# Sparse graph attention on one core: order of the setup, of the first softmax and of the last group's stores, and one lag for the V products

## The chip, the core and the metric

The kernel runs on one core of a Trainium2 chip. A core has five engines that run side by side, each with its own queue of instructions, taken in order: TensorE (PE, with its weight loads as PEld), VectorE (DVE), ScalarE (ACT), GpSimd (POOL) and SyncE (SP). SyncE, ScalarE and GpSimd can issue DMAs. The metric is the device time of one execution in microseconds; the time of a kernel is the median of several executions.

## What is computed

A graph of 3327 nodes with 256 features each goes through four layers. `adj` has about 0.5% ones, some 16 neighbours a row. Layer 0 is a graph attention whose score depends on the row alone; layers 1 to 3 are transformer layers with 8 heads of 32, in which node n attends to its neighbours only.

```
# layer 0
h = x @ Wt.T + bt
s = leaky_relu(h @ Wa.T + ba)                      # one number a row
w = softmax(where(adj > 0, s, -9e15), axis=1)
x = layernorm(x + (w @ h) @ Wp.T + bp)
# layers 1, 2, 3
q, k, v = split(layer_norm(x) @ w_qkv)
scores  = where(adj != 0, q @ k.T / sqrt(32), -inf)   # for each head
x = x + (softmax(scores) @ v) @ w_proj + b_proj
x = x + gelu(layer_norm(x) @ w1 + b1) @ w2 + b2
```

## The kernel before

The rows are 26 blocks of 128, in 7 groups of four blocks (the last group has two). All instructions are in an order written out by hand: what stands first in the program on an engine is issued first there, and waits for its inputs with everything behind it waiting too. The kernel has two stages.

**Setup and adjacency (first 470 us).** For each block i of `adj`: `load` brings its 128 rows in (SyncE), `sign` turns them into bf16 0/1 on ScalarE (L722; three buffers), `turn` transposes them with 26 matmuls on TensorE and four copies on ScalarE (L731, L732), `candidates` and `list` find the neighbours' numbers on VectorE (L743, L747; L753 to L760). `sums(i)` multiplies the turned pair of blocks with h, split in bf16 parts, on TensorE (L869, L871).

Before the loop, x itself has to be turned and multiplied into h: for each group `x_turn(g)` (L803, copies L805) and one step later `h_of(g - 1)` (matmuls L813, an add on VectorE L819). Between these steps stand `pieces`: the candidates and lists of blocks 2, 3 and 4, cut into five pieces each, for VectorE. `turn(3)` stands after group 2's step, `sign` of block 4 in group 4's. Then come `sum_h` (L840), `split_h` (L828 to L834), `sums(1)`, `turn(4)`, `sums(3)`, the copy of group 0's sums, `turn(5)`, `back` of group 0 and `sums(5)`.

In the loop, i goes from 4 to 25; each i has a first half (load and sign of block i + 2, then the steps of `plan[2 * i]`, candidates of block i) and a second (turn of block i + 2, sums after every second one, the steps of `plan[2 * i + 1]`, list of block i). The plan spreads what each group needs after its sums: copy and back (ScalarE and TensorE), `soft` (small VectorE operations L903 to L932 and two exps on ScalarE, L933 and L934), `mix` (VectorE, L952 to L964, needs the exps), `place`, `project` (TensorE s_ptn and s_pp, ScalarE s_nT), `add` (VectorE, L985, needs s_pp), norms, `turn1` and the products for Q, K and V of layer 1 (`qkv`, L1023), and `store`. Group 0 has all its steps one half later than the other groups.

After the loop the last two groups are finished. `store` and `qkv` put K and V rows into the table kv[1] (L1029) and the rows of x, Q and neighbour lists into the table t1 (L1035, L1036); ScalarE issues these DMAs. Block ranks by degree give the permutation `perm` (L1199 to L1207); `wide` carries the ranks into kv[1] (L1171, ScalarE).

**Layers 1 to 3.** GpSimd gathers rows of kv by neighbour number, four neighbours of 128 nodes at a time: a tile `kv` of a ring of 10 buffers (L1325, four gathers a tile; in layer 1 also 26 gathers of t1's rows, L1285). For each tile, `scores` multiplies with Q and reduces on VectorE (L1347, L1348). After a block's last tile `softmax` finds the maximum on VectorE (L1359) and takes the exp on ScalarE (L1362), followed there by `take_q` of the next block (L1333). Later `weights` (L1368 to L1375) and, for each tile, `values` multiply V with the weights on VectorE (L1388) and add up on TensorE (L1394) into po; that frees the tile and lets GpSimd gather the next one (`issue`). `block` then projects (L1418) and adds (L1422); every few blocks a `chunk` runs the norm, the feed-forward part (L1462, L1468, L1485, L1499, L1503) and the next layer's Q, K, V (L1515, L1521 to L1523) in steps that `some` hands out after each tile. After all blocks the next layer's gathers start, since they read rows that this layer wrote.

When the V products of a block may start is set in `run`: at least one tile of the next block must have been scored in the last layer and for block 0, at least two elsewhere. One V product is done for each scored tile, two when more than five tiles wait for theirs.

Of the kernel before, what the change touches and what calls it, by code (L numbers as in the profile page):

```python
# [8 lines left out]
FP = mybir.dt.float32  # L9
BF = mybir.dt.bfloat16  # L10
I32 = mybir.dt.int32
# [6 lines left out]
P = 128  # L18
N = 3327
D = 256  # L20
HEADS = 8
HD = D // HEADS
# [26 lines left out]
LMAX = CAPS[0]  # L49
# [474 lines left out]
def sparse_path(ctx, tc, ins, out, dram, flag):  # L524
    nc = tc.nc
# [15 lines left out]
    t1 = dram.tile([PADDED, T1W], FP, name="t1")  # L541
    kv = {1: dram.tile([PADDED + 1, KVW[1]], FP, name="kv1"),
          2: dram.tile([PADDED, KVW[2]], FP, name="kv2"),
          3: dram.tile([PADDED, KVW[3]], FP, name="kv3")}
# [21 lines left out]
    class Norm:  # L566
# [18 lines left out]
        def turn(self, j, v, work, pb):  # L585

            xn = work.tile([P, D], FP, tag="xn", name=f"xn_{self.name}_{j}")
            nc.scalar.activation(xn, v, AF.Identity, bias=self.nm[:, j:j + 1],  # L588
                                 scale=self.rs[:, j:j + 1])
            for c in range(2):  # L590
                nc.tensor.transpose(pb[c][:, j * P:(j + 1) * P], xn[:, c * P:(c + 1) * P], ident)  # L591
# [31 lines left out]
    with tc.tile_pool(name="a", bufs=1) as a, tc.tile_pool(name="aw", bufs=2) as aw, \  # L623
# [4 lines left out]
        def bank(name):  # L628
            return a_ps.tile([P, 512], FP, tag="bank", name=name)
# [25 lines left out]
        x_sb = a.tile([P, NB, D], FP, name="s_x")  # L655
# [27 lines left out]
        lists = a.tile([P, NB, LMAX], FP, name="lists")  # L683
# [124 lines left out]
        def h_of(g):  # L808
            blocks, xT = GROUPS[g], turned.pop(g)
            ph = bank(f"s_ph_{g}").rearrange("p (b h) -> p b h", h=H0)  # L810
            for j, i in enumerate(blocks):
                for c in range(2):
                    nc.tensor.matmul(ph[:, j, :], xT[:, c, j * P:(j + 1) * P],  # L813
                                     S.wtT[:, c, :], start=(c == 0), stop=(c == 1))
            full = [j for j, i in enumerate(blocks) if ROWS[i] == P]
            for j0, j1, r in ((0, len(full), P), (len(full), len(blocks), ROWS[-1])):
                if j1 > j0:
                    i0 = blocks[j0]
                    nc.vector.tensor_add(  # L819
                        S.h[:r, i0:i0 + j1 - j0, :], ph[:r, j0:j1, :],  # L820
                        S.bt_b[:r, None, :].to_broadcast([r, j1 - j0, H0]))
# [14 lines left out]
        def sum_h():  # L836
            ph = bank("s_phsum")
            for i in range(NB):
                r = ROWS[i]
                nc.tensor.matmul(ph[:, :H0], ones[:r, :], S.h[:r, i, :],  # L840
                                 start=(i == 0), stop=(i == NB - 1))
            S.hsum = a.tile([P, H0], FP, name="s_hsum")
            nc.scalar.copy(S.hsum, ph[:, :H0])
# [11 lines left out]
        class Group:  # L855
# [150 lines left out]
            def turn1(self):  # L1006
# [4 lines left out]
                    self.n1.turn(j, x_sb[:, i, :], aw, pb)  # L1011
                self.n1.out(self.hT, pb, S.w1["g1"], S.w1["be1"])

            def qkv(self, j0):

                if j0 == 0:
                    self.ql = aw.tile([P, 4, D + LMAX], FP, tag="ql", name=f"ql_{self.g}")
                for j in range(j0, min(j0 + 2, self.n)):
                    i = self.blocks[j]
                    pk, pq = bank(f"s_pk_{i}"), bank(f"s_pq_{i}")  # L1020
                    for ps, c0, c1 in ((pk, D, 3 * D), (pq, 0, D)):
                        for c in range(2):
                            nc.tensor.matmul(ps[:, :c1 - c0], self.hT[:, c, j * P:(j + 1) * P],  # L1023
                                             S.w1["w_qkv"][:, c, c0:c1],
                                             start=(c == 0), stop=(c == 1))
                    kvr = aw.tile([P, 2 * D], FP, tag="kvr", name=f"s_kvr_{i}")
                    nc.scalar.copy(kvr, pk)
                    nc.scalar.mul(self.ql[:, j, :D], pq[:, :D], -HD ** -0.5)
                    nc.scalar.dma_start(kv[1][1 + i * P:1 + (i + 1) * P, :2 * D], kvr)  # L1029
# [11 lines left out]
        groups = [Group(g) for g in range(len(GROUPS))]  # L1041
        blk = [Block(i) for i in range(NB)]
# [18 lines left out]
        for i in range(2):  # L1061
# [6 lines left out]
        pieces = [lambda i=i, k=k: blk[i].candidates(k) if k < 4 else blk[i].list()  # L1068
                  for i in (2, 3, 4) for k in range(5)]
        NG = len(GROUPS)  # L1070
        for g in range(NG):
            x_turn(g)
            if g == 1:

                for _ in range(5):
                    pieces.pop(0)()
            if g:
                h_of(g - 1)
                pieces.pop(0)()
            if g == 2:  # L1080
                turn(3)
            if g == 4:
                blk[4].load()
                blk[4].sign()
        h_of(NG - 1)
        sum_h()
        split_h()
        blk[5].load()
# [17 lines left out]
        for g in reversed(range(NG)):  # L1106
            at = dict(zip(names, (0, 1, 3, 4, 5, 5, 6, 7, 8, 9, 10, 11, 12)))
            first = 8 * g + 4
            if g == 0:
                first = 8  # L1110
                at = {k: v + 1 for k, v in at.items()}
                at["copy"] = at["back"] = -9
            elif g == NG - 2:
                at.update(norm=6, norm1=7, turn1=7, qkv0=99, qkv2=99, store=99)
            elif g == NG - 1:
                first = 2 * NB - 4
                at.update(soft=2, mix=3, place=3, project=3, add=99, norm=99, norm1=99, turn1=99, qkv0=99,
                          qkv2=99, store=99)
            for name in names:
                k = first + at[name]  # L1120
                if 0 <= k < 2 * NB:
                    plan[k].append((g, name))

        def step(g, name):
            G = groups[g]
            G.qkv(int(name[3:])) if name[:3] == "qkv" else getattr(G, name)()

        for i in range(4, NB):
            if i + 2 < NB:
                blk[i + 2].load()  # L1130
                blk[i + 2].sign()
            for s in plan[2 * i]:
                step(*s)
            if i > 4:
                blk[i].candidates()
            if i + 2 < NB:
                turn(i + 2)
                if i % 2 or i + 2 == NB - 1:
                    sums(i + 2)
            for s in plan[2 * i + 1]:  # L1140
                step(*s)
            if i > 4:
                blk[i].list()
        last = groups[-2:]
# [23 lines left out]
        nc.vector.tensor_add(rank, rank, r2)  # L1168
        wide = a.tile([P, NB, KVW[1] - 2 * D], FP, name="wide")
        nc.vector.tensor_copy(wide, rank[:, :, None].to_broadcast(list(wide.shape)))  # L1170
        nc.scalar.dma_start(kv[1][1:, 2 * D:].rearrange("(b p) c -> p b c", p=P), wide)  # L1171

        last[1].norm1()
        last[1].turn1()
        last[1].qkv(0)
        last[1].store()


        hib = aw.tile([P, NB, NB], BF, tag="abf", bufs=3, name="hib")
# [19 lines left out]
        for i in range(NB):  # L1199
            nc.tensor.matmul(pp[:, :2 * NB], oh_lo[:, i, :],  # L1200
                             ids[:, i, :, :].rearrange("p a b -> p (a b)"),
                             start=(i == 0), stop=(i == NB - 1))
# [19 lines left out]
        d = 0  # L1222
        while d < nd:
# [4 lines left out]
            d = e  # L1228
# [62 lines left out]
    CHUNK, at = {}, 0  # L1291
# [7 lines left out]
    class Layer:  # L1299
# [282 lines left out]
        def run(self):  # L1582
            L = self.L
            for _ in range(NBUF):
                self.issue()
            self.take_q(ORDER[0])

            todo, wait = [], {}
            def value():
                if todo[0][1] == 0:  # L1590
                    self.weights(todo[0][0])
                self.values(*todo.pop(0))

            for k, b in enumerate(ORDER):

                behind = 1 if self.nxt is None or b == 0 else 2
                for g in slots[b]:
                    self.scores(*g)
                    if g == slots[b][-1]:
                        self.softmax(b)  # L1600
                        if k + 1 < NB:
                            self.take_q(ORDER[k + 1])
                    for i in wait:
                        wait[i] += 1
                    for _ in range(2 if len(todo) > NBUF // 2 or b == 0 else 1):
                        if todo and wait[todo[0][0]] >= behind:
                            value()
                    self.some()
                todo += slots[b]
                wait[b] = 0  # L1610

            table = small.tile([P, HEADS], FP, tag="table", name=f"table_{L}")
            nc.scalar.activation(table, ident[:, :HEADS], AF.Gelu_apprx_tanh)
            while todo:
                value()
            self.rate = 4.0
            while self.short or self.long or self.stores:
                self.some()
# [45 lines left out]
```

## Time and profile before

| what | us |
|---|---|
| median of 3 runs | 3120.58 |
| lowest, highest | 3101.62, 3137.48 |
| the profiled execution | 2503.21 |
| its span, first to last instruction | 2501.4 |
| first scores of layer 1, 2, 3 in it | 486.59, 1174.51, 1862.17 |

The profiled execution is one execution, 617 us faster than the median of the timed ones; durations below are from it. Lines of a timeline give start, length, engine, line of the kernel, operation, output <- input, shapes and count; in brackets stands how long the engine had been idle before it and what ended that wait. Lines of a list of waits give who waited for whom, the total, how often, and the longest wait. Names: s_a is the adjacency as it was loaded, s_abf its sign, s_aT the turned block, s_pa and s_pc the sums, s_m the two softmax terms of layer 0, s_pp the projection, kv the gathered tile, vw the weighted V, po the block's output, pu, py and pd the feed-forward products. A matmul of f32 operands shows as several instructions.

### The profile page before, as it was taken

Reading aid. Unit: us, or ns where it says so; the run is one execution under the profiler, and the core shown is the slowest. Engines: PE = TensorE matmul, PEld = TensorE weight load, DVE = VectorE, ACT = ScalarE, POOL = GpSimd, SP = SyncE. Lnnn points to the kernel's source line nnn. Section 1 sums busy time; section 2 is a strip of 40 time slices with the busy share of each in tenths; the row PEclk is TensorE's granted clock in tenths of the full one; section 3 lists DMA queues with packets and bytes.
Section 4 is the critical chain, followed back from the end, with each engine's and each line's share of the span. In section 5 each row is a group of like instructions: output and inputs, shape, how many; then the busy total and the mean of one; then the engine's idle time right before and its main releaser. Section 6 shows DMA issues by size and latency. Waiting matters only on the chain.

```text
span 2501.4 us, 24067 instructions
## 1 busy us (share of the span) xinstructions
PE 1667.9 (67%) x7561; PEld 1120.1 (45%) x7561; DVE 1937.5 (77%) x3984; ACT 783.8 (31%) x1324; POOL 1361.8 (54%) x1458
## 2 busy tenths in 40 slices
PE   6767775336677877774367778787743666766667
PEld 5745553134454544543244445444432443444444
DVE  6798999577898887763788888867637878788874
ACT  6456563102333333332023233333220221322222
POOL 5000000377777776632777767656327777777771
PEclk9878776658798888887587888888875778877888
DMA  6325420677877776654777767756437767667762
GB/s 266 132 91 199 144 90 35 205 217 218 230 227 217 228 227 186 191 113 134 210 211 215 215 185 212 211 163 185 103 121 210 211 187 209 200 201 206 206 192 51
DMA packets 144630, 453.80 MB, mean 181 GB/s; under 512 B 29537, under 2 KB 40172, under 8 KB 141293
## 3 DMA queue, kind: packets, MB, share of 16 engines
q0 software_dynamic: 113056, 370.26, 52.0%
q1 hardware_dynamic: 9978, 53.90, 6.0%
q10 hardware_dynamic: 21458, 28.02, 3.1%
q8 instruction: 61, 1.00, 0.2%
q14 instruction: 77, 0.63, 0.1%
HBM read 420.64 MB, written 31.42 MB: 181 GB/s over the span
## 4 chain that ended last, share of the span: by engine, by line
PE 19%; DVE 17%; DMA 11%; POOL 7%; issue 7%; ACT 2%; DVEq 0%; ACTq 0%; POOLq 0%
DMA kv<-kv,t 10%; POOL kv L1325 7%; PE pu L1462 6%; PE py L1485 4%; PE po L1394 4%; DVE kv L1347 4%; DVE vw L1388 4%; DVE sc L1348 3%; PE pk L1515 2%; PE po L1418 1%; DVE st_n L575 1%; PE pq L1515 1%; DVE t L1503 1%; DVE den L1368 0%; PE py L1478 0%
## 5 line engine op out<-in xcount | busy, mean ns | idle before, releaser
L1325 POOL DMA_INDIRECT kv<-kv,t x1344 | 1273.1, 947 | 641.8 <-issue 349.9
L1394 PE MATMUL po<-s_ident,vw 128*128 128x128 f32 x2688 | 454.0, 327 | 492.9 <-DVE vw L1388 491.6
L1394 PEld LDWEIGHTS po<-s_ident,vw 128*128 128x128 f32 x2688 | 380.2, 169 | 619.4 <-DVE vw L1388 518.2
L1347 DVE TENSOR_TENSOR kv<-kv,q 128x1024 f32<-128x1024 f32 (+3 forms) x363 | 413.5, 1139 | 280.4 <-DMA kv<-kv,t 150.7
L1348 DVE TENSOR_REDUCE sc<-kv 128x32 f32<-128x1024 f32 (+3 forms) x363 | 414.1, 1141 | 12.4
L1388 DVE TENSOR_TENSOR vw<-kv,w 128x1024 f32<-128x1024 f32 x333 | 372.4, 1128 | 1.8
L1462 PE MATMUL pu<-fT,s_w 128*128 128x512 f32 (+2 forms) x768 | 321.6, 554 | 2.9 <-ACT fT L596 2.9
L1485 PE MATMUL py<-gT,s_w 128*128 128x512 f32 (+1 forms) x672 | 283.7, 550 | 0.0
L1468 ACT ACTIVATE gT<-pu,pvb 128x512 f32<-128x512 f32 (+2 forms) x192 | 116.2, 608 | 351.7 <-PE pu L1462 351.0
L1462 PEld LDWEIGHTS pu<-fT,s_w 128*128 128x128 f32 x768 | 151.7, 212 | 122.0 <-issue 87.7
L717 POOL MEMSET s_abf<- 128x1 bf16 x23 | 2.2, 106 | 332.4 <-DVE s_v L743 205.8
L1485 PEld LDWEIGHTS py<-gT,s_w 128*128 128x128 f32 x672 | 124.8, 192 | 105.0 <-issue 67.8
L747 DVE MAX8 cand<-s_v 128x8 f32<-128x208 bf16 x416 | 118.0, 361 | 0.9
L1515 PE MATMUL pk<-s_w_qkv,nT 128*128 128x512 f32 x208 | 111.4, 662 | 6.0 <-ACT nT L596 6.0
L588 ACT ACTIVATE xn_f<-t,nm_f,rqy_f 128x256 f32<-128x256 f32 x78 | 43.2, 594 | 218.3 <-DVE nm_f L582 211.6
L591 PE MATMUL pf<-s_ident,xn_f 128*128 128x128 f32 x156 | 45.9, 435 | 95.3 <-ACT xn_f L588 95.2
L1362 ACT ACTIVATE sc<-sc,mx 128x120 f32<-128x120 f32 (+6 forms) x78 | 32.0, 410 | 239.8 <-DVE mx L1359 239.3
L1418 PE MATMUL po<-s_w_proj,oT 128*128 128x256 f32 x312 | 101.9, 459 | 0.0
L731 PE MATMUL s_ptb<-s_ident_bf,s_abf 128*128 128x128 bf16 x676 | 66.8, 264 | 51.3 <-ACT s_abf L722 32.3
L732 ACT COPY s_aT<-s_ptb 128x896 bf16<-128x896 bf16 x104 | 82.3, 859 | 34.0 <-PE s_ptb L731 34.0
L731 PEld LDWEIGHTS <-s_abf 128*128 128x128 bf16 x676 | 56.3, 121 | 64.8 <-ACT s_abf L722 38.0
L1412 ACT COPY oT<-po 128x256 f32<-128x256 f32 x78 | 28.9, 370 | 176.0 <-PE po L1394 175.5
(290 smaller groups left out, 2235.0 us busy)
## 6 DMA issues: line engine op xcount, KB each, us to landing
s_a<-in_adj_dram SPq DMA_DIRECT2D x24, 1663.5 KB
kv<-kv,t POOLq DMA_INDIRECT x1344, 3.7
kv<-kvr ACTq DMA_DIRECT2D x52, 256.0 KB
kv<-s_kvr ACTq DMA_DIRECT2D x26, 256.0 KB
s_w<-in_L_gnn_w_dram SPq DMA_DIRECT2D x6, 1024.0 KB
t<-ql ACTq DMA_DIRECT2D x6, 592.0 KB
t<-s_x ACTq DMA_DIRECT2D x6, 512.0 KB
s_w_qkv<-in_L_gnn_w_qkv_dram SPq DMA_DIRECT2D x3, 768.0 KB
```

Of the source, the lines that this page charges most:

```text
L731: nc.tensor.transpose(pt[:, m, :], self.abf[:, k * P:(k + 1) * P], ident_bf)
L747: nc.vector.max(out=self.cand[:, s, :], in_=self.v[:, s, :])
L1325: nc.gpsimd.indirect_dma_start(out=t[:, s, :], out_offset=None, in_=kv[L], in_offset=bass.IndirectOffsetOnAxis(ap=t2[:, b, k:k + 1].bitcas ...
L1347: nc.vector.tensor_mul(k, k, self.q[b][:, None, :].to_broadcast([P, n, D]))
L1348: nc.vector.tensor_reduce(self.sc[b][:, s0:s0 + n, :], k.rearrange("p s (h d) -> p s h d", d=HD), AX.X, ALU.add)
L1388: nc.vector.tensor_mul(vw[:, :n * D].rearrange("p (s h d) -> p s h d", h=HEADS, d=HD), v, self.wp[b][:, s0:s0 + n, :, None].to_broadcast([ ...
L1394: nc.tensor.matmul(self.po[b][:, k * P:(k + 1) * P], vw[:, at:at + P], ident, is_transpose=True, start=(s0 + s == 0 and k == 0), stop=(s0 ...
L1418: nc.tensor.matmul(ps, c["oT"][:, k * P:(k + 1) * P], w["w_proj"][:, k, :], start=False, stop=(k == 1))
L1462: nc.tensor.matmul(c["pu", f][:, :n], w["w1"][:, e, f * P:(f + 1) * P], c["hT"][:, e, :n], start=(e == 0), stop=(e == 1))
L1468: nc.scalar.activation(g[:, :n], c.pop(("pu", f))[:, :n], AF.Gelu_apprx_tanh, bias=w["b1"][:, f:f + 1])
L1485: nc.tensor.matmul(c["py"][e][:, :n], w["w2"][:, f, e * P:(e + 1) * P], g[:, :n], start=(f == 0), stop=last)
L1515: nc.tensor.matmul(ps[:, :c1 - c0], c["hT"][:, e, j * P:(j + 1) * P], nxt["w_qkv"][:, e, c0:c1], start=(e == 0), stop=(e == 1))
```

## The change

Four things change, all of order or issuer; no product is added or left out.

1. In the setup, `turn(3)` and the sign of block 4 move behind the last `h_of`, and the last group's step no longer takes a piece; five pieces are left for later instead of four.
2. Group 0's steps lose their extra half, so each stands half a block earlier. Its `soft` leaves the plan: it runs in the loop at i = 5 after the candidates, and block 7's sign is put behind it.
3. `wide` is issued by SyncE. The last group's `qkv` and `store` become `q_first`: the lists are copied and the rows of x stored first, Q of both blocks is multiplied before K and V, copied at once and stored, then K and V are copied and stored. SyncE issues these five DMAs.
4. In `run` the V products of every block may start when one tile of the next block has been scored.

```diff
+            def of_x(self, ps, j, c0, c1):
+                for c in range(2):
+                    nc.tensor.matmul(ps[:, :c1 - c0], self.hT[:, c, j * P:(j + 1) * P],
+                                     S.w1["w_qkv"][:, c, c0:c1], start=(c == 0), stop=(c == 1))
+
+            def q_first(self):
+                g, n, b0 = self.g, self.n, self.blocks[0]
+                self.ql = aw.tile([P, 4, D + LMAX], FP, tag="ql", name=f"ql_{g}")
+                nc.vector.tensor_copy(self.ql[:, :n, D:].bitcast(I32), lists[:, b0:b0 + n, :])
+                rows = t1[b0 * P:(b0 + n) * P, :].rearrange("(b p) c -> p b c", p=P)
+                nc.sync.dma_start(rows[:, :, :D], x_sb[:, b0:b0 + n, :])
+                pq = bank(f"s_pq_{g}").rearrange("p (b d) -> p b d", d=D)
+                pk = [bank(f"s_pk_{i}") for i in self.blocks]
+                for j in range(n):
+                    self.of_x(pq[:, j, :], j, 0, D)
+                for j in range(n):
+                    self.of_x(pk[j], j, D, 3 * D)
+                nc.scalar.mul(self.ql[:, :n, :D], pq[:, :n, :], -HD ** -0.5)
+                nc.sync.dma_start(rows[:, :, D:], self.ql[:, :n, :])
+                for j, i in enumerate(self.blocks):
+                    kvr = aw.tile([P, 2 * D], FP, tag="kvr", name=f"s_kvr_{i}")
+                    nc.scalar.copy(kvr, pk[j])
+                    nc.sync.dma_start(kv[1][1 + i * P:1 + (i + 1) * P, :2 * D], kvr)
...
             if g:
                 h_of(g - 1)
-                pieces.pop(0)()
-            if g == 2:
-                turn(3)
+                if g < 6:
+                    pieces.pop(0)()
             if g == 4:
                 blk[4].load()
-                blk[4].sign()
         h_of(NG - 1)
+        blk[4].sign()
+        turn(3)
         sum_h()
...
             if g == 0:
                 first = 8
-                at = {k: v + 1 for k, v in at.items()}
-                at["copy"] = at["back"] = -9
+                at["copy"] = at["back"] = at["soft"] = -9
...
             if i + 2 < NB:
                 blk[i + 2].load()
-                blk[i + 2].sign()
+                if i != 5:
+                    blk[i + 2].sign()
             for s in plan[2 * i]:
                 step(*s)
             if i > 4:
                 blk[i].candidates()
+            if i == 5:
+                groups[0].soft()
+                blk[i + 2].sign()
...
-        nc.scalar.dma_start(kv[1][1:, 2 * D:].rearrange("(b p) c -> p b c", p=P), wide)
+        nc.sync.dma_start(kv[1][1:, 2 * D:].rearrange("(b p) c -> p b c", p=P), wide)
 
         last[1].norm1()
         last[1].turn1()
-        last[1].qkv(0)
-        last[1].store()
+        last[1].q_first()
...
             for k, b in enumerate(ORDER):
-
-                behind = 1 if self.nxt is None or b == 0 else 2
                 for g in slots[b]:
...
-                        if todo and wait[todo[0][0]] >= behind:
+                        if todo and wait[todo[0][0]] > 0:
                             value()
```

More of the change, by code (lines that the diff above doesn't have):

```diff
@@ L1021, in qkv @@
                     for ps, c0, c1 in ((pk, D, 3 * D), (pq, 0, D)):
[L1022 to L1025, printed above, removed]
+                        self.of_x(ps, j, c0, c1)
                     kvr = aw.tile([P, 2 * D], FP, tag="kvr", name=f"s_kvr_{i}")
```

## The prediction

> **What bounds the kernel now.** I read the page first, then the busy time cut into stages, then VectorE's waits in each stage, then the timeline around the longest one. The page:
>
> ```profile
> span 2501.4 us, 24067 instructions
> PE 1667.9 (67%) x7561; PEld 1120.1 (45%) x7561; DVE 1937.5 (77%) x3984; ACT 783.8 (31%) x1324; POOL 1361.8 (54%) x1458
> ```
>
> VectorE is the busiest, but 77% is a mean over stages with different limits. Busy time by stage (columns: PE, PEld, DVE, ACT, POOL, granted clock, DMA share and rate):
>
> ```profile
> 107.00:120.00 13.00, 10.72 (x102) 9.82 (x103) 0.00 (x0) 8.99 (x8) 0.00 (x0) 0.74 0.56 200
> 120.00:440.00 320.00, 215.20 (x1414) 159.76 (x1412) 295.25 (x1092) 171.01 (x227) 4.49 (x17) 0.75 0.32 112
> ...
> 1175.00:1370.00 195.00, 103.19 (x420) 73.33 (x421) 153.53 (x234) 35.64 (x66) 146.07 (x156) 0.68 0.73 214
> 1370.00:1775.00 405.00, 309.36 (x1223) 193.00 (x1222) 333.87 (x576) 129.79 (x215) 270.53 (x287) 0.84 0.67 195
> ```
>
> To see: in the loop over adjacency blocks (120 to 440 us) VectorE is busy 295 of 320 us and so sets the pace; just before it there is a stretch in which VectorE does nothing at all. The timelines of VectorE and ScalarE say why:
>
> ```profile
> 120.28 0.16 DVE L952 TENSOR_TENSOR s_z<-deg,s_m 128x4 f32<-128x4 f32 x1 [13.57 <-ACT s_m L933]
> ```
> ```profile
> 105.97 3.01 ACT L722 ACTIVATE s_abf<-s_a 128x3327 bf16<-128x3327 int32 x1
> 110.00 1.71 ACT L732 COPY s_aT<-s_ptb 128x896 bf16<-128x896 bf16 x2 [1.02 <-PE s_ptb L731]
> 111.90 1.50 ACT L732 COPY s_aT<-s_ptb 128x896 bf16<-128x896 bf16 x2 [0.19 <-PE s_ptb L731]
> 113.28 2.99 ACT L722 ACTIVATE s_abf<-s_a 128x3327 bf16<-128x3327 int32 x1
> 119.08 0.59 ACT L878 COPY s_sa<-s_pa 128x512 f32<-128x512 f32 x1 [2.81 <-PE s_pa L869]
> ...
> 120.04 0.21 ACT L933 ACTIVATE s_m<-s_m 128x4 f32<-128x4 f32 x1
> ```
>
> The first group's two exps are queued behind two signs, four copies of a turn and the copy of group 1's sums. In the attention layers the waits of VectorE differ; layer 2 from 1370 to 1770 us, and layer 3 (which already follows the rule that the change extends):
>
> ```profile
> DVE kv L1347 <- ACT q L1333: 33.3, 12, 6.8
> DVE t L1503 <- PE pd L1499: 13.0, 2, 8.3
> DVE t L1422 <- PE po L1418: 12.4, 8, 2.2
> ```
> ```profile
> DVE kv L1347 <- DMA kv<-kv,t: 75.4, 51, 7.2
> ...
> DVE den L1368 <- ACT sc L1362: 0.6, 1, 0.6
> ```
>
> In the middle of layer 2 VectorE never waits for a gather: it waits for ScalarE and TensorE. Gathers bind only at a layer's start (26.1 us of such waits from 1175 to 1370) and end.
>
> **What the Trainium skill says.** "DVE: scalar operands, raw-bit mode, write accounting and state across instructions", section 5, calls VectorE's queue one in-order queue; the trace agrees, since the list of block 6 stood ready behind the mix for those 13.57 us. "DMA: Bandwidth & Descriptors", section "Issuing engines are not separate DMA queues", says that DMAs of all issuers share 16 engines and another issuer saves only the time of initiating. Here that is 0.34 us (L1029) to 1.11 us (L1171) on ScalarE each. "TensorE: Matmul & The Clock Gate", Part 1, says that the array halves its clock after idling and recovers when busy; the sums that start at 75.83 after two idle waits (2.52 and 2.71 us) step at 0.21 us and then at 0.11.
>
> **Part 1, turns of x (setup).** 26 transposes (3.4 us of TensorE from 47.64) leave the chain of x turns, with sign(4), 2.98 us of ScalarE at 57.10. The last s_ph then ends near 64.5 - 3.4 = 61; VectorE, whose list of block 3 ends about 62, can start split_h near 63 rather than 68.7. But 3.4 us of candidates of block 4 went behind it, so VectorE gains 2.5. What is late next: turn(3)'s copies are behind sign(4) (63.5 + 3.1), so s_phsum runs 65.6 to 71.6, and sums(1) begin at 71.6 instead of 75.83, without the idle. I take TensorE 5 us earlier from here.
>
> **Part 2, first softmax.** With of_h at 84 and candidates(5) to 90.8, soft (2.4) and list(5) (3.7) VectorE is done at 97. The exps come after turn(6)'s copies (end 106.1 - 5 = 101), and before sign(7), turn(7), sign(8), copy(1). Mix waits 4 us instead of 13.57. But group 0's later steps also move half a block forward: its add now stands ahead of candidates(7), and its s_pp needs, after 101, sign(7) 3.0, turn(7) 4.4, sums(7) 5.7, copy(1) 1.2, back and nT 3.4, first s_pp 1.2 = 120, while VectorE (mix 2.5, candidates 6.4, place 0.7, list 3.7) arrives at 115: a new wait of about 5. Other groups stand at this place already, and one of them waited 4.33 us (s_x L985 from s_pp, at 229.30). Sum of parts 1 and 2: -13.6 + 4 + 5 - 2.5 = -7. VectorE-bound afterwards, so it stays. Bounds: -16 (neither wait) to -2 (7 us each).
>
> **Part 3, last group.** The stage ends like this:
>
> ```profile
> 463.55 0.45 ACTq L1036 DMA_DIRECT2D t<-ql  x1
> 466.89 0.07 DVE L1253 MEMSET least<- 128x8 f32 x1 [0.19 <-DMA t<-ql]
> 467.27 0.24 SPq L608 DMA_DIRECT2D colsb<-in_L_gnn_g_dram  x1
> 468.17 0.97 POOL L1285 DMA_INDIRECT t<-t,perm  x1 [90.36 <-DMA colsb<-in_L_gnn_be_dram]
> ```
>
> Wide's issue (1.11 us, 451.48) leaves ScalarE, which then starts turn1 at 451.5, not 452.64: -1.2 for the products, perm and VectorE's end (466.7). Four more issues (2 x 0.34, 0.38, 0.45) leave it too, and Q goes first: ql can leave near 458.5, five us earlier. All of them go into SyncE's in-order queue ahead of load_rest's loads; SyncE issued nothing from 344 to 467.27, and the last kvr copy is done by 462, so it isn't held. The ql landing is then no longer last, but VectorE reads that stage's buffers to 465.5, and t2 and the weight tiles lie in the memory that it frees. So weights, row gathers and first scores (486.59) come 1.3 earlier. Bounds: -5 if the gathers needn't wait for that memory (perm near 462.4), +1 if SyncE is held.
>
> **Part 4, V.** Counted through run(): under the old rule a block's first group after the softmax has no V, and todo over 5 makes two at the next block's start. The new rule makes 53 of a layer's 121 V products one group earlier and none later; po's steps and the chunk steps keep their turns. Ring buffers come free up to four gathers (4 x 1.25 us) earlier. At a layer's start GpSimd runs at its 1.25 us pitch without standing, so no buffer is missing: nothing. In the middle VectorE waits for q, po and pd, not gathers: nothing. At the end of layer 2 GpSimd stands 7.81 us at 1745.90 and VectorE later waits 8.5 us for gathers; that goes, but the add at 1799.24 then waits longer than its 9.69 us for TensorE. I take -1 per layer, a V inside the pd wait at 1736.34 (4.67). Bound: -8.5 per layer. No new wait for exp: take_q of the next block is queued behind it and the next scores wait for q; layer 3 shows 0.6 us.
>
> **Sum.** -7 - 1.3 - 2 = -10 against the profiled execution, 2503.2 us. The median of the timed runs is 3120.6, 617 us more, which no view explains; I scale the gain by 1 to 1.25 and take -12: **3109 us**.
>
> **Rivals.** *All stays saved* (chance 0.18): -16 - 5 - 17 = -38, scaled -42: 3078. For it: loop and layer start are bound where the gain lies; against it: s_pp's wait and the pd wait at 1799. *Nothing shows* (0.12): in the timed runs something slower than VectorE bounds the stage: 3120. *Slower: V holds TensorE* (0.17): 12 blocks a layer (24, 1, 23 to 13) had no V in their first turn, so chunk transposes and projection ran there at once; now they are queued behind a V that waits for scores, weights and product. At 2.2 us each (the longest po wait) 2 x 12 x 2.2 = +53: 3173; against my -12 it makes the kernel slower from 0.5 us each. Against it: layer 3 with this rule waits for po 1.8 us and pd 6.8 in all. *The forecast* has 0.53. That V doesn't move at all is excluded by the count in part 4, though 68 of 121 products stay where they were.
>
> **Numbers.** About 1% (31 us) is what a measurement of this kernel can tell from no change; runs before lie 36 us apart. Forecast and nothing-shows fall within: same 0.65; faster 0.18; slower 0.17. Range 3078 to 3140: from the second case to the forecast's weak end (no gain) and half the spread of runs; it leaves out the slow rival.
>
> **What would show it.** Right: s_z's wait 13.57 falls to some 4, a wait of s_x for s_pp of some 5 appears near 120, the loop ends 7 us earlier, first scores near 478, q waits and layers 1 and 2 unchanged within 3 us. Wrong: s_pp without wait (part 2 too small), first row gather by 456 (t2 not held), po or pd waits in regular chunks grown, SyncE's first load later than VectorE's end, GpSimd's stall ending a layer.

## The result, and the profile after

The kernel after took 3137.7 us (median of 20 executions, 3120.8 to 3164.1), the kernel before 3119.7 beside it (20 executions, 3101.6 to 3137.5). The ratio is 1.0066, 95% interval 1.0046 to 1.0086. The forecast was 12 us faster; the change made the kernel 18 us slower.

The kernel before takes some 2502 us at some times and 3120 to 3128 us at others, so each run below stands beside the kernel before of its own time, and the traces laid beside the profile before (2503 us) are those of the faster times. The change measured there, under the label f0_after, took 2529.6 us against 2502.6, ratio 1.0098 (1.0081 to 1.0114), which is 27 us. The page of that run (span and instructions, then busy time by engine):

```profile
span 2531.7 us, 24072 instructions
PE 1700.8 (67%) x7561; PEld 1145.4 (45%) x7561; DVE 1940.5 (77%) x3984; ACT 783.6 (31%) x1323; POOL 1362.5 (54%) x1458
```

To see: VectorE does the same work as before (1940.5 us against 1937.5), but TensorE needs 33 us more for as many matmuls (1700.8 against 1667.9, x7561 both times). Nothing was added to it; it worked more slowly.

Where the loss lies, from the start of some instructions (us; before is the fresh profile e0_before; these two executions are 31 us apart, 4 more than the medians):

| stage | before | after (f0_after) | difference |
|---|---|---|---|
| candidates of the last block begin | 415.4 | 435.0 | +19.6 |
| from there to layer 1's first scores | 70.2 | 69.9 | -0.3 |
| layer 1, first scores to layer 2's | 687.5 | 692.0 | +4.5 |
| layer 2, first scores to layer 3's | 687.8 | 694.5 | +6.7 |
| layer 3, first scores to the end | 639.8 | 640.2 | +0.4 |

Two places lose: the setup and loop, which parts 1 and 2 touch, and layers 1 and 2, which part 4 touches. VectorE's waits in the loop, from 84 to 420 us, first before, then after (columns: who waited for whom, us in total, times, longest):

```profile
DVE s_z L952 <- ACT s_m L933: 13.4, 1, 13.4
DVE s_x L985 <- PE s_pp L976: 5.7, 4, 4.3
DVE s_v L743 <- ACT s_abf L722: 0.3, 1, 0.3
```
```profile
DVE s_x L985 <- PE s_pp L976: 14.5, 5, 6.9
DVE deg L903 <- ACT s_acc L890: 7.5, 1, 7.5
DVE s_z L952 <- ACT s_m L933: 7.1, 2, 4.3
```

To see: the one wait of 13.4 us for the exps is gone as forecast (2.82 us at 118.61 is what is left of it), but the waits sum to 29.1 us instead of 19.4. The other half of the 19.6 us lies ahead of this window. VectorE's waits from 43 to 84 us, first before, then after:

```profile
DVE s_h L819 <- PE s_ph L813: 10.1, 4, 5.3
```
```profile
DVE s_h L819 <- PE s_ph L813: 19.0, 6, 5.5
```

### The profile page after: what moved, and what is told of

It reads as the page before. It is cut to its first block, busy times and chain, and to the rows that moved or that the text cites. A ratio compares the mean times of both kernels' runs of the same rounds, so it can differ in the third digit from the quotient of the medians.

```text
span 3126.0 us, 24072 instructions
## 1 busy us (share of the span) xinstructions
PE 1792.0 (57%) x7561; PEld 1181.4 (38%) x7561; DVE 1936.6 (62%) x3984; ACT 780.4 (25%) x1323; POOL 1364.2 (44%) x1458
## 4 chain that ended last, share of the span: by engine, by line
issue 15%; POOL 14%; PE 11%; DVE 8%; another core or an unknown queue 6%; DMA 2%; ACT 2%; ACTq 0%; DVEq 0%; POOLq 0%
POOL kv L1349 14%; PE pu L1486 3%; PE po L1418 2%; DMA kv<-kv,t 2%; PE py L1509 2%; DVE kv L1371 2%; DVE vw L1412 2%; DVE sc L1372 1%; PE pk L1539 1%; PE po L1442 1%; PE pf L591 0%; PE pq L1539 0%; PE py L1502 0%; ACT xn_f L588 0%
## 5 line engine op out<-in xcount | busy, mean ns | idle before, releaser
L1418 PE MATMUL po<-s_ident,vw 128*128 128x128 f32 x2688 | 485.1, 337 | 567.0 <-DVE vw L1412 366.1
L1418 PEld LDWEIGHTS po<-s_ident,vw 128*128 128x128 f32 x2688 | 401.8, 176 | 707.3 <-DVE vw L1412 359.7
L1486 PE MATMUL pu<-fT,s_w 128*128 128x512 f32 (+2 forms) x768 | 347.1, 588 | 101.6 <-ACT gT L1492 62.0
L1509 PE MATMUL py<-gT,s_w 128*128 128x512 f32 (+1 forms) x672 | 315.5, 596 | 51.3 <-ACT gT L1492 26.5
L1446 DVE TENSOR_TENSOR t<-t,po 128x256 f32<-128x256 f32 x78 | 32.6, 418 | 340.0 <-remote 195.4
L1509 PEld LDWEIGHTS py<-gT,s_w 128*128 128x128 f32 x672 | 132.5, 205 | 179.1 <-issue 103.9
L1539 PE MATMUL pk<-s_w_qkv,nT 128*128 128x512 f32 x208 | 121.4, 712 | 20.9 <-ACT nT L596 12.4
L1442 PEld LDWEIGHTS po<-s_w_proj,oT 128*128 128x128 f32 x312 | 72.2, 256 | 151.1 <-issue 140.2
L1527 DVE TENSOR_TENSOR t<-t,pd 128x256 f32<-128x256 f32 x75 | 29.4, 404 | 158.6 <-PE pd L1523 152.4
L1442 PE MATMUL po<-s_w_proj,oT 128*128 128x256 f32 x312 | 110.2, 490 | 0.0
```

The costliest lines, as they stand in the source:

```text
L1418: nc.tensor.matmul(self.po[b][:, k * P:(k + 1) * P], vw[:, at:at + P], ident, is_transpose=True, start=(s0 + s == 0 and k == 0), stop=(s0 ...
L1442: nc.tensor.matmul(ps, c["oT"][:, k * P:(k + 1) * P], w["w_proj"][:, k, :], start=False, stop=(k == 1))
L1486: nc.tensor.matmul(c["pu", f][:, :n], w["w1"][:, e, f * P:(f + 1) * P], c["hT"][:, e, :n], start=(e == 0), stop=(e == 1))
L1509: nc.tensor.matmul(c["py"][e][:, :n], w["w2"][:, f, e * P:(e + 1) * P], g[:, :n], start=(f == 0), stop=last)
L1539: nc.tensor.matmul(ps[:, :c1 - c0], c["hT"][:, e, j * P:(j + 1) * P], nxt["w_qkv"][:, e, c0:c1], start=(e == 0), stop=(e == 1))
```

## The experiments

### The parts, one by one and together

Each of these runs is the kernel before with the named parts of the diff above and nothing else: e0_before none, e4_v_alone part 4, e5_without_v parts 1 to 3, e6_without_turns parts 2 to 4, f0_after all. What was expected:

> The kernel before, once more, for a profile of an execution of the usual length beside the one of 2503 us. All theories: ratio 1.000 within 0.003. If the 617 us between that profile and the timed runs is one stage, one interval between marks (end of the adjacency loop, first scores of each layer, end) grows by it; if it is a slower engine everywhere, all grow by about a quarter. The profile of the kernel after suggests the second: its three layers last 910, 872 and 834 us against 688, 688 and 639, and VectorE's add L1422 waits on average 3.6 us beyond the recorded end of its projection on TensorE, against 0.1 us in the fast profile. So I expect such gaps here too, in the kernel before, and layers of about 890, 870 and 830 us.

> Only part 4 (V one tile behind the exp in all blocks). Theory V (the V products ahead of a block's chunk steps hold TensorE, which in usual executions is later than in the fast profile): ratio 1.006 or more, 19 us or more, with layers 1 and 2 longer by some 10 us each and the setup unchanged. Theory SETUP (the turns of x without the sign and turn(3) between them, or the first softmax, cost the time): ratio 1.000 within 0.002. Forecast as on record: 0.999.

> Parts 1, 2 and 3 together, without part 4. Theory V: ratio 0.997 (the 7 + 1.3 us forecast for these parts are saved, and nothing is lost). Theory SETUP: 1.006, the end of the adjacency loop later by some 18 us, layers unchanged.

> Parts 2, 3 and 4 without part 1 (turn(3) and the sign of block 4 stand between the turns of x, as before). Theory V: 1.006, as the whole change. Theory SETUP in the form that the order of part 1 is what costs: 0.999 or below; in the form that the first softmax costs: 1.006, with group 0's waits in the loop to show for it.

> The kernel after the change, unchanged, beside the same runs of before as its parts. If the parts add (V alone +6, parts 1 to 3 +15 us): ratio 1.008 to 1.009, 21 us; the adjacency loop ends 16 to 20 us later than before, layers 1 and 2 are 3 us longer each. If they overlap: 1.005 to 1.006.

| run | parts | median us | before | ratio, 95% interval |
|---|---|---|---|---|
| e0_before | none | 2503.9 | 2502.4 | 1.0002 (0.9994 to 1.0010) |
| e4_v_alone | 4 | 2507.9 | 2502.4 | 1.0026 (1.0017 to 1.0036) |
| e5_without_v | 1, 2, 3 | 2517.8 | 2502.4 | 1.0057 (1.0040 to 1.0074) |
| e6_without_turns | 2, 3, 4 | 2515.3 | 2502.4 | 1.0051 (1.0038 to 1.0064) |
| f0_after | all | 2529.6 | 2502.6 | 1.0098 (1.0081 to 1.0114) |

Neither theory held alone. Part 4 costs 0.26%, with layers 1 and 2 longer by 3.8 and 3.3 us where some 10 each were expected; the setup parts cost 0.57%, and the sum, 0.83%, is within the interval of the whole: the losses add. The expectation for e0_before, that its stages would be a quarter longer, was wrong; it ran like the profile before.

### Part 1: the sign and turn(3) behind the last h_of

e1_turns_alone is part 1 alone. e8_turns_filled puts TensorE instructions where turn(3) stood, without ScalarE's copies, and nobody reads them:

```diff
+            if g == 2:
+                for k0 in range(0, NB, 7):
+                    pt = a_tp.tile([P, 8, P], BF, tag="tp", name=f"s_idle_{k0}")
+                    for m, k in enumerate(range(k0, min(k0 + 7, NB))):
+                        nc.tensor.transpose(pt[:, m, :], blk[2].abf[:, k * P:(k + 1) * P], ident_bf)
             if g == 4:
                 blk[4].load()
```

e13_turns_filled_twice does the same with 52 transposes.

> Only part 1. Theory CLOCK (the 26 transposes of turn(3) between the turns of x gave TensorE an unbroken stretch, after which it works at twice the rate; without them it stays at half rate through the products of x, s_phsum and the first sums): products of h at 0.213 us a step until about 88 us instead of 0.112 from 52 us, sums(1) end near 95 instead of 82, ratio 1.004 to 1.006. Theory ORDER (sign(4) and turn(3)'s copies are only behind something else now, the rate is as it was): sums(1) end within 3 us of before and the ratio is 1.000. Forecast as on record for this part: 2.5 to 5 us earlier.

> Part 1 with 26 transposes of block 2 put where turn(3) stood, whose result nobody reads; everything else as in part 1 alone. Theory CLOCK: the rate doubles near 52 us as in the kernel before, s_phsum ends before 72 us, and the ratio falls from 1.004 to 1.006 for part 1 alone to 1.000 or below, although TensorE has 26 instructions more. Theory ORDER: 3 us later than part 1 alone, 1.005 to 1.007.

> Part 1 with 52 transposes without a reader where turn(3) stood, twice as many as in the run before, so that TensorE works without a gap from the third group's products of h to the next turn of x, some 9 us. In the run with 26, eleven executions took 2494 to 2502 us and three 2517. Theory CLOCK: with 52 the high ones go; all executions lie below part 1 alone (2504 to 2519), the ratio is 0.997 to 1.000, although 26 more instructions stand in the queue. Theory ORDER (the rate is chance, and filling doesn't decide it): the spread stays as in part 1 alone, and the added 2.8 us show: 1.003 to 1.005.

| run | median us | lowest to highest | ratio, 95% interval |
|---|---|---|---|
| e1_turns_alone | 2510.6 | 2504.6 to 2519.4 (19) | 1.0028 (1.0019 to 1.0037) |
| e8_turns_filled | 2498.4 | 2494.0 to 2517.5 (14) | 0.9996 (0.9977 to 1.0016) |
| e13_turns_filled_twice | 2497.3 | 2488.7 to 2504.8 (22) | 0.9982 (0.9972 to 0.9992) |

Groups of TensorE's instructions from 43 to 78 us (line, operation, out<-in, shapes, count | busy us, mean ns of one | idle time before them), in e0_before, e1_turns_alone and e13_turns_filled_twice:

```profile
L813 PE MATMUL s_ph<-s_wtT,s_xT 128*128 128x64 f32 x88 | 12.3, 301 | 0.1
```
```profile
L813 PE MATMUL s_ph<-s_wtT,s_xT 128*128 128x64 f32 x88 | 19.9, 422 | 1.4 <-ACT s_xT L805 1.4
```
```profile
L813 PE MATMUL s_ph<-s_wtT,s_xT 128*128 128x64 f32 x88 | 12.6, 304 | 1.2 <-ACT s_xT L805 1.2
L1085 PE MATMUL s_idle<-s_ident_bf,s_abf 128*128 128x128 bf16 x52 | 4.3, 263 | 0.0
```

To see: the same 88 products take 7.6 us more when turn(3) is away, and are back at their time when something without a use stands in its place. From start to start they step at 0.213 us or at 0.112. Before, they step at 0.112 from 52.08 us on. In e1_turns_alone TensorE stops for some 0.7 us after every four turns of x, since the next ones wait for ScalarE's copy, and stays at half rate until 76.9. In f0_after it stays there through s_phsum as well, and sums(1) end at 96.0 instead of 82.7. The group s_phsum in e0_before and in f0_after:

```profile
L840 PE MATMUL s_phsum<-s_h,s_ones 128*128 128x64 f32 (+1 forms) x52 | 6.0, 275 | 0.0
```
```profile
L840 PE MATMUL s_phsum<-s_h,s_ones 128*128 128x64 f32 (+1 forms) x52 | 11.3, 421 | 0.0
```

That the transposes bring the rate is shown inside one row: of the 52 equal transposes of e13_turns_filled_twice, from 47.08 on, those up to 49.6 step at 0.107 us, those after at 0.056. The granted clock of that run changes with them, at 49.68 (columns as in the prediction's table by stage; the granted clock is the third from the end):

```profile
36.00:48.00 12.00, 10.98 (x56) 10.31 (x55) 9.87 (x33) 4.28 (x7) 3.66 (x4) 0.50 0.78 296
48.00:62.00 14.00, 12.82 (x125) 11.87 (x123) 4.92 (x18) 3.99 (x9) 0.10 (x1) 0.94 0.02 5
```

It is not that TensorE needs a stretch without a hole, as the expectation for e1_turns_alone has it. In f0_after TensorE works from 63.2 to 92.3 us with no hole over 0.25 us and stays at half rate; products with 64 columns (s_ph, s_phsum) fill most of that time. The clock records of the traces show what goes with a change. A trace's records begin with its first change to full rate (51.58 us in e0_before, 76.86 in e1_turns_alone, 92.38 in f0_after), and the granted clock reads 1.00 ahead of it, whatever the rate. All changes lie whole multiples of 3.413 us apart; the first three distances in e0_before are 20.48, 6.83 and 27.31 us, that is 6, 2 and 8 times. This agrees with the Trainium skill, "TensorE: Matmul & The Clock Gate", Part 1, which says that activity is judged in windows of 3.4 us that run freely. What the window ahead of a change holds is the same in all eighteen traces: up to 100 us, at least 2.5 us of turns (of the adjacency or of x), filling transposes or bf16 sums. Not every window with as much is followed by a change. Two windows of f0_after, 78.73 to 85.56 us, are full of s_phsum alone, and the rate stays.

So where a window's edge falls decides too. From the last products of h to the start of s_phsum, f0_after and e1_turns_alone give TensorE the same instructions at nearly the same times. In f0_after an edge, at 75.32 us, divides turn(3) (73.71 to 76.95), and the rate stays; in e1_turns_alone nearly all of turn(3) lies in the window from 73.45 to 76.86, and the rate doubles at its end. The edge differs from one execution to the next: in the profile of e4_v_alone, whose setup is that of the kernel before, TensorE was at full rate from 37.75 us. This would explain why the executions with 26 filling transposes are of two kinds, eleven from 2494 to 2502 us and three at 2517, and those with 52 are not: 52 take 5.5 us at half rate (an estimate, 52 times 0.107), so half of them still fill most of a window. It is not shown, since the one profiled execution with 26 was at full rate from 37.4 us, before its transposes.

Theory CLOCK thus holds in that removing the transposes costs the rate: with the rate kept, part 1 gains 4.2 us, where the forecast had 2.5 to 5; without it, the part loses 8. The order of the copies and the sign isn't what cost. For part 1 alone the theory's figures were too high: the ratio is 1.0028 and not 1.004 to 1.006, and sums(1) end at 88.7 and not near 95.

### Part 2: the first softmax and the half block

e9_soft_only moves `soft` and block 7's sign as the change does, but leaves group 0's other steps half a block later, as before; e2_first_softmax is part 2 as it stands. The line in which e9 differs from part 2:

```diff
                 first = 8
-                at["copy"] = at["back"] = at["soft"] = -9
+                at = {k: v + 1 for k, v in at.items()}
+                at["copy"] = at["back"] = at["soft"] = -9
```

> Of part 2 only the first softmax ahead of block 7's sign; group 0's other steps keep their extra half block. Theory HALF (what part 2 loses comes from the other steps standing half a block earlier, ahead of their TensorE results): the wait of s_z falls from 13.4 to under 4 us, a wait of deg for s_acc of about 4 stays, s_x does not wait 7 us for s_pp, the loop ends 4 to 8 us earlier and the ratio is 0.997 to 0.999. Theory SOFT (the early softmax itself only moves the wait on): the loop ends within 2 us of before or later, 1.000 to 1.003.

> Part 2 alone, which so far is only a difference of other runs: parts 2, 3, 4 took 12.9 us more and part 4 alone 6.5, the softmax without the half block 4.7 us less. Theory HALF: part 2 alone costs 6 to 8 us, ratio 1.0025 to 1.003, so that the half block of the other steps costs some 11 to 13; the waits of s_acc, s_z and s_pp of group 0 sum to about 13.7 us, as much as the one wait of 13.4 before, and one of s_x for s_pp near 235 us grows from 4.3 to over 7. Theory SUM (the parts only disturb each other): 0.999 to 1.000.

e9_soft_only: 2497.8 us against 2502.6, ratio 0.9983 (0.9977 to 0.9990). e2_first_softmax: 3136.3 against 3127.7, ratio 1.0024 (1.0002 to 1.0046). The early exps gain 4.7 us; the half block takes more than that back. VectorE's waits in the loop with the softmax alone:

```profile
DVE s_x L985 <- PE s_pp L976: 10.2, 5, 4.1
DVE deg L903 <- ACT s_acc L890: 5.5, 2, 3.8
```

15.7 us instead of 19.4, and no wait for the exps at all; the last candidates begin 3.4 us earlier, where 4 to 8 were expected. With the half block too (e6_without_turns, where part 1 does not disturb) they sum to 25.9: group 0 has 3.9 (deg), 2.8 (s_z) and 7.0 (s_x at 126), as much together (13.7) as the wait for the exps that went, and group 2's s_x then waits longer; e0_before, then e6_without_turns:

```profile
228.09 0.69 DVE L985 TENSOR_TENSOR s_x<-s_x,s_pp 128x512 f32<-128x512 f32 x1 [4.31 <-PE s_pp L976]
```
```profile
234.38 0.69 DVE L985 TENSOR_TENSOR s_x<-s_x,s_pp 128x512 f32<-128x512 f32 x1 [7.61 <-PE s_pp L976]
```

The cause of that second wait stands some 40 us earlier. ScalarE's queue and TensorE's in e6_without_turns (L1049 and L1016 are the copies and products of `qkv`, L1027 and L1023 before):

```profile
186.05 0.58 ACT L1049 COPY s_kvr<-s_pk 128x512 f32<-128x512 f32 x1 [4.57 <-PE s_pk L1016]
...
189.93 2.98 ACT L722 ACTIVATE s_abf<-s_a 128x3327 bf16<-128x3327 int32 x1
```
```profile
192.96 1.68 PE L731 MATMUL s_ptb<-s_ident_bf,s_abf 128*128 128x128 bf16 x14 [3.51 <-ACT s_abf L722]
```

To see: half a block earlier, group 0's second qkv step stands behind the sums, and the next block's sign behind its copies, which wait 4.57 us for TensorE. TensorE then stands 3.51 us for that sign, and its turn starts at 192.96, at half rate; before, it starts at 187.98, since the sign (182.55) was ahead of these copies. The back products and group 2's exps and s_pp are 5 us late with it. In e2_first_softmax the same five waits are there (2.8 and 4.3 for s_z, 3.5 for deg, 6.8 and 6.3 for s_x). Theory HALF holds, though the wait of s_x expected to grow to "over 7" there measured 6.3.

### Part 4: the V products

First the waits of VectorE in layer 2, from its first scores to layer 3's, the wait of some 7 us ahead of these included: before, with part 4 alone, and with the V products behind the turn's steps (below):

```profile
DVE kv L1347 <- DMA kv<-kv,t: 42.8, 18, 7.3
DVE t L1503 <- PE pd L1499: 22.2, 4, 9.0
DVE t L1422 <- PE po L1418: 16.4, 10, 3.6
```
```profile
DVE kv L1347 <- DMA kv<-kv,t: 36.3, 16, 7.1
DVE t L1503 <- PE pd L1499: 29.3, 4, 14.4
DVE t L1422 <- PE po L1418: 20.5, 15, 3.6
```
```profile
DVE kv L1347 <- DMA kv<-kv,t: 36.5, 18, 7.2
DVE t L1503 <- PE pd L1499: 28.1, 4, 15.2
...
DVE t L1422 <- PE po L1418: 11.9, 6, 3.6
```

To see: part 4 does what it says, 6.5 us of waiting for gathers go. But VectorE waits 7.1 us more for pd, most of it at the layer's end, and 4.1 more for po, fifteen times instead of ten, and layer 2 is 3.3 us longer (691.1). What po waits for is seen in one turn of layer 1:

```profile
971.73 0.37 ACT L1412 COPY oT<-po 128x256 f32<-128x256 f32 x1
...
979.27 1.94 PE L1394 MATMUL po<-s_ident,vw 128*128 128x128 f32 x8 [6.46 <-DVE vw L1388]
...
981.22 1.91 PE L1418 MATMUL po<-s_w_proj,oT 128*128 128x256 f32 x4
```

The finished block's oT is ready at 972.10, yet its projection starts at 981.22: ahead of it in TensorE's queue stand the sums of the next block's first V, which wait 6.46 us for VectorE. Before, the projection of this turn starts 0.65 us after its copy. The line of it in e0_before:

```profile
976.76 1.03 PE L1418 MATMUL po<-s_w_proj,oT 128*128 128x256 f32 x4
```

The projection also runs at half rate now (1.91 us for four instead of 1.03): TensorE has stood, and the granted clock is half from 976.41.

Two runs change only this place. e12_v_behind_steps issues a V that the new rule brings forward behind the steps of its turn; e16_v_sums_behind issues only TensorE's sums there and leaves VectorE's product ahead.

```diff
+                    late = 0
                     for _ in range(2 if len(todo) > NBUF // 2 or b == 0 else 1):
                         if todo and wait[todo[0][0]] >= behind:
                             value()
+                        elif todo and wait[todo[0][0]] > 0:
+                            late += 1
                     self.some()
+                    for _ in range(late):
+                        value()
```

> Part 4 alone, but a V product that the new rule brings forward is issued behind the steps of that turn (block's projection, chunk), not ahead of them. The count of V products a turn is the same. Theory HOLD (the V product stands ahead of the steps on VectorE and TensorE and makes them later): the loss of 1.0026 goes, 0.999 to 1.000, and the waits of VectorE for pd and po return from 28 and 18 us a layer to 22 and 15. Theory SPREAD (V products that come earlier leave TensorE less to do at a time, and it falls to half rate oftener, wherever they stand): the loss stays, 1.002 to 1.003, with as many products at half rate.

> Part 4 alone, with VectorE's product of a V brought forward ahead of the turn's steps (as in the change), but TensorE's sums of it behind them. With both behind, the ratio was 0.997, with both ahead 1.0026. If it is TensorE's queue in which they hold the steps: 0.996 to 0.998, with po waits near 12 us a layer. If it is VectorE's queue: 1.001 to 1.003, with po waits near 18.

e12_v_behind_steps: 2494.9 us against 2501.5, ratio 0.9970 (0.9959 to 0.9981). e16_v_sums_behind: 3111.8 against 3127.7, ratio 0.9951 (0.9923 to 0.9979). Theory HOLD holds, and e16 points to TensorE's queue: with the sums behind, the same V products gain what they cost ahead, wherever VectorE's product stands. Two things stay open there: V ahead of the steps was not run beside 3127.7, so its loss is known only beside 2502; and the expected po waits of 12 us can't be checked, since in layer 2 of e16 22.4 us of the add's waits are put down to po and 43.6 more to no engine. Layer 2 of e12 takes 680.9 us instead of 687.8. One expectation fell: the pd wait stays at 28.1, so the steps' place did not make it. By its size (5.9 us more than before) it is the gathers' wait (6.3 less) that moved to the next thing that is late, which no run tests; the gain comes through po, 11.9 us instead of 20.5. The half rate takes part in it: of the 78 distances between a block's four projection matmuls in layer 2, 15 are over 1.6 times the usual 0.215 us before, 24 with V ahead, 12 with V behind.

### The parts in the form that does not lose

e10_soft_last is the softmax without the half block and part 3; e11_soft_last_warm adds 40 transposes without a reader right behind turn(2); e15_mended_no_turns is e10 with the V products behind the steps; e14_all_mended adds part 1 with 52 filling transposes.

> Only what has been seen to gain or is free: the early softmax with group 0's other steps left where they were, and part 3. If the two add: the softmax's -4.7 us and -1 us for part 3, ratio 0.997 to 0.998. If part 3 costs something that the sum of other parts hid: 0.999 or above.

> The same, with 40 transposes of block 2 without a reader right behind turn(2), in the time in which TensorE stands for the parameters' rows (29.8 to 33.7 us). Theory CLOCK: 26 + 40 transposes without a gap bring the full rate before the turns of x, which then step at 0.11 us from the start; the last h_of ends 3 to 4 us earlier and the ratio is 0.0015 below that of the run without them. If the rate is lost again in the gaps that follow, or the rows come later behind them: equal, or 1 to 2 us later.

> The same without part 1. If the gains add: -4.3 for softmax and part 3 and -6.6 for V, ratio 0.9955 to 0.9965, and the run with part 1 filled is 2 to 4 us faster; if filled part 1 and the softmax share their gain, both are equal.

> All four parts, each in the form that did not lose: part 1 with 52 filling transposes (-4.2 us alone), the first softmax without the half block (-4.7), part 3, and V brought forward behind the turn's steps (-6.6). If they add: 2486 to 2489 us, ratio 0.994 to 0.995. If part 1 and the softmax share one wait of VectorE (s_z, 11.9 us with part 1 filled): 0.995 to 0.996.

| run | median us | before | ratio, 95% interval |
|---|---|---|---|
| e10_soft_last | 2497.3 | 2501.5 | 0.9985 (0.9976 to 0.9994) |
| e11_soft_last_warm | 2498.6 | 2501.5 | 0.9982 (0.9975 to 0.9989) |
| e15_mended_no_turns | 3107.7 | 3127.7 | 0.9929 (0.9905 to 0.9954) |
| e14_all_mended | 3104.0 | 3127.7 | 0.9930 (0.9903 to 0.9957) |

Part 3 adds nothing that timing shows over the softmax alone (0.9983). In the profiles, the way from the last candidates to the first scores is 67.6 to 69.9 us in the five runs with part 3 beside 2502 and 69.9 to 72.5 in the seven without it; the medians are 0.8 us apart, where 1.3 was forecast. Warming early failed: TensorE was at full rate only from 34.8 to 38.3 us, while the products of the parameters' rows ran. From 41.3, when x's copies came, the turns stepped at half rate until 55.3, and the first of them came 3.6 us later. The last two are 20 and 24 us faster than the kernel before; 0.7% is more than the gains beside 2502 add up to (0.15% and 0.30%), as V alone gave 0.49% beside 3127.7. What part 1 adds to the softmax there can't be told: the two runs differ by 3.7 us, which their intervals cover. That the two parts share one gain, as one expectation has it, is not shown.

## Why the prediction was wrong, point by point

- **Its case.** The chain that the forecast followed, VectorE's, was the right one, and the waits that it meant to remove went or shrank. Three of the four parts were spoilt by results of TensorE that came later, which the forecast took at a fixed rate and at a fixed place in the queue. That 3137.7 us still lies within its range (to 3140) is luck: this end of the range stood for no gain and the spread of runs, not for a loss.
- **Part 1, the step that failed first.** "The last s_ph then ends near 64.5 - 3.4 = 61". It subtracts turn(3)'s 3.4 us and keeps the duration of what is left. The add that needs it started at 73.95 (f0_after): the 26 transposes had brought TensorE to full rate, and without them what is left ran at half of it. The text before had shown the two rates itself, for the sums that follow two idle waits, and did not ask what the removal of the transposes does to them. With the rate kept, the 2.5 to 5 us of this step were right (4.2).
- **Part 2.** The wait of s_z, "4 us instead of 13.57", measured 2.8; the new wait for s_pp, "of about 5", 6.8 to 7.0. Not foreseen: soft stands behind deg's copy of s_acc (3.9 us, 7.5 when part 1 makes TensorE late). "VectorE-bound afterwards, so it stays" failed: the half block put the second qkv step's copies ahead of a sign, and group 2 lost 6 us more at 213 to 236 us. I had followed the moved steps up to s_pp and not their ScalarE copies, 60 us later in the plan.
- **Part 3.** SyncE was free, and the first row gather didn't move ahead of VectorE's end (485.80 us after 485.14 in f0_after), as forecast. The 1.2 us for perm did not come with the whole change: from the last candidates to perm it is 46.8 us in f0_after as in e0_before. They came in e10_soft_last and e11_soft_last_warm (45.2 and 45.1).
- **Part 4.** "po's steps and the chunk steps keep their turns" is true and was the wrong question: within the turn they moved behind a V. The rival *V holds TensorE* names the mechanism that e12 and e16 show. Its price was 2.2 us for each of 12 blocks, though the blocks that it lists are 13; 3.3 us more a layer is 0.25 for each, below the 0.5 from which it was to decide, and it decided only together with the setup. Layer 3, which was held against it, was a poor witness: 1.8 us of po waits there say nothing of layers with chunks that also make the next layer's Q, K and V.
- **The scaling.** A factor of 1 to 1.25 on the gain was no help: the change costs 27 us beside 2502.6, the profile's own time, and 18 beside 3119.7. The 617 us between them are, as far as two profiles of the kernel after show (the last section), spread over all three layers and not in one stage.

## What to carry to other kernels

Instructions taken out from between dependent TensorE instructions may have been what brought the engine to full rate: look in several traces at what stands in the last microseconds ahead of the change of rate, and if it is what you remove, take the durations of the rest at half rate. When a step is moved ahead, look in each in-order queue at what stands directly behind it and at what it will wait for there: here a V product's sums waited for VectorE ahead of a projection that was ready, and putting them behind it turned a loss of 0.26% into a gain of 0.3%. When parts of a change can be run alone, test each with one thing put back before dropping it; three of these four were good in another form.

## What the runs showed of the hardware that was not expected

- A stretch in which TensorE always works is not enough for full rate: in f0_after it stays at half rate from 63.2 to 92.3 us with no hole over 0.25 us, on products with 64 columns for the most part, and doubles behind a window of bf16 sums alone (88.97 to 92.38).
- The granted clock follows this rate, but only from a trace's first change on: in the windows from 48 to 69 us it reads 1.00 in f0_after, whose records begin at 92.38 and whose products step at 0.213 us, while from 36 to 48 us it reads 0.50 in e13_turns_filled_twice, whose records begin at 22.38. Ahead of the first change the distance from start to start is the measure.
- One kernel, two times: in the profile of the result the layers of the kernel after take 910, 872 and 834 us against 692, 695 and 640 in f0_after, and the first scores come at 510 and 505 us. In the longer one VectorE's adds that wait start on average 3.6 us after the recorded end of their projection (47 cases, up to 18.8 us), in f0_after 0.11 us. What makes the difference is left open.
